# Two cross-attentions in f32 on one core: the second layer's products joint over two pairs of subtiles, and its softmax by head on ScalarE

## The chip, the core and the metric

One core of one Trainium2 chip runs the whole kernel. The metric is the device time of one execution in microseconds (us). The engines are named as in the profile: PE (TensorE, matrix products; PEld is its weight load), DVE (VectorE), ACT (ScalarE), POOL (GpSimd), SP (SyncE, which only issues transfers here). SBUF is the on-chip memory of 128 partitions, PSUM the accumulator memory that PE writes. PSUM holds eight banks of 512 f32 in each partition.

## The reference

x has 4 batches of 1024 tokens, 1024 wide: 4096 rows. ctx has 64 rows a batch, S = 64. All is f32.

```python
# layer 0, 32 query heads on 8 key heads
q, k, v = x @ Wq + bq, ctx @ Wk + bk, ctx @ Wv + bv
attn = softmax(q k^T / sqrt(32) + mask)          # per head
z  = (attn v) @ Wo + bo + x
x1 = layernorm(z, eps=1e-6) * gamma + beta
# layer 1, 16 heads of 64
a = layernorm(ctx, eps=1e-5) * ln_gamma + ln_beta
Q, K, V = x1 @ Wq.T, a @ Wk.T, a @ Wv.T
attn = softmax(where(mask, Q K^T / 8, -inf))     # per head
y = x1 + tanh(gate) * ((attn V) @ Wo.T)
```

## The kernel before

**The folding.** With only 64 context rows, layer 1 needs two square weights per batch: `ad[b]` (1024x1024) is Wq folded with K, so that the scores of all 16 heads are x1 · ad[b], and `bd[b]` is V folded with Wo and the gate, so that y = x1 + p · bd[b], with p the softmax of 16 heads x 64 columns. Both are made during layer 0 and kept in DRAM.

**Winograd's seven products.** Each large product is a one-level Strassen-Winograd product of 2x2 blocks. A subtile is 128 rows; a *pair* is two subtiles (256 rows), whose two subtiles are the two row blocks of the left factor; its 1024 columns, and the weight's rows and columns, are halved. `left_out` makes the left factor's sums S1, S2, S3, S4 on DVE (four instructions of 128x512, lines 429 to 432), `right_sums` those of the weight, T1, T2, T3, N4 (four of 128x2048, lines 183 to 186). `products` then runs seven products, each of four matmuls of 128x512 with f32 (line 446; the trace has two records for one of them), into PSUM banks, and `add` brings each bank to the result in SBUF with a DVE instruction (line 455, or line 459 where the key's mask is added as a bias). `project` runs a list of other work, the `fill`, in seven parts behind the seven steps. In the order of the code the products are:

```python
("X", "A11", "B11", ...), ("X", "S2", "T2", ...), ("V", "S3", "T3", ...), ("X", "S1", "T1", ...),
("X", "S4", "B22", ...), ("V", "A22", "N4", ...), ("W", "A12", "B21", ...)
```

Below they are called P1, P6, P7, P5, P3, P4 and P2 in that order (the same numbers as the changed code has).

**Layer 1.** There are 16 pairs, four a batch. Call S the product that gives a pair's scores, and R the one that gives its y. The order is S0, S1, R0, S2, R1, S3, ..., S15, R14, R15, so that a softmax has an R phase to be made in. For S, the rows x1 come from DRAM by quarters (`load_x1`, SP's queue) in a layout in which DVE's 32x32 stream transpose turns them (`turn_quarters`, line 419), and `left_out` follows. The softmax of a subtile is on DVE: maximum (L493), a clamp (L498), the subtraction of the maximum over 128x1024 (L501), then exp of the whole 128x1024 on ACT (L502), and on DVE the sum (L511), the reciprocal (L512) and the multiplication (L516). p goes to DRAM (`p1`) and comes back by quarters (`turn_p`), both over ACT's queue. For pairs 0 and 15 p is not sent to DRAM: PE turns it by 16 transposes each (`turn_at_once`, line 407) and ACT copies the result (L414). Residual rows x1 are loaded over SP's queue into four buffers `res1`, in which R adds, and y is stored from there.

At each new batch `right_weight` loads a new weight (16 transfers) and DVE makes its four sums: a's in R, b's in S.

**PSUM and order.** `ps_wx` has four single banks, `ps_big` two double ones. Buffers are of pools that rotate: a new tile waits until the last reader of the old one is done. Instructions of each engine run in an order that is fixed when the program is built (a scheduler merges the steps of the code by their dependences); at run time each engine follows its own list and waits on semaphores. DMA issues stand in the lists of the engines that issue them.

**Layer 0 near its end.** `project` of pair 15 is the last product, and then the layer norm of its two subtiles (`close_rows`, `normalize_steps`) and their stores to x1 run as `fill`. `other_work` loads bo for layer 0's GpSimd add of bias and residual rows (L962), and `open_stage` loads gamma and beta. x1[0] and x1[1] are loaded and turned during layer 0's last pairs.

Of the kernel before, what the change touches and what calls it, by code (L numbers as in the profile page):

```python
# [14 lines left out]
P = 128  # L15
# [56 lines left out]
def tile_two_cross_attentions(  # L72
# [27 lines left out]
    def sub_ap(t):  # L100
        return slice(t * P, (t + 1) * P)
# [5 lines left out]
    small = ctx.enter_context(tc.tile_pool(name="small", bufs=4))  # L107
    ps_wx = ctx.enter_context(tc.tile_pool(name="ps_wx", bufs=4, space=bass.MemoryType.PSUM))
    ps_big = ctx.enter_context(tc.tile_pool(name="ps_big", bufs=2, space=bass.MemoryType.PSUM))

# [122 lines left out]
    def constant(ap, shape, name, dt=F32, pool=const):  # L233
        t = pool.tile(shape, dt, tag=name, name=name)
        nc.sync.dma_start(out=t, in_=ap)
        return t
# [5 lines left out]
    beta1_sb = constant(beta1, [P, KC], "beta1")  # L242
    mask1_sb = constant(mask1.partition_broadcast(P), [P, B, S], "mask1", U8)
    gate_sb = constant(gate.partition_broadcast(P), [P, 1], "gate")
# [400 lines left out]
    def load_queries(t):  # L645
        q = qpool.tile([P, KC, P], F32, tag="q", name=f"q0_{t}")
        nc.sync.dma_start(out=q, in_=qTd[t // SUB][:, :, sub_ap(t % SUB)])

        m = small.tile([P, 2, S], F32, tag="m0", name=f"m0_{t}", bufs=2)
        for e in range(2):  # L650
            nc.sync.dma_start(out=m[:, e], in_=mask0[sub_ap(t), :])
        queries[t] = q, m
# [313 lines left out]
    def other_work(rows):  # L966

        nonlocal fold, early, bo_sb, w_o, first, first_rows, second
        for blk in range(1, NBLK):
# [18 lines left out]
        w_o, w_o_loads = right_loads(wo0, "wa", "wo0", "heads")  # L988
        bo_sb = constant(bo0.partition_broadcast(P), [P, H], "bo", F32, fold)
        for k in range(KC):  # L990
# [49 lines left out]
    def open_stage():  # L1040
        nonlocal lpool, o2pool, rpool, gamma0_sb, beta0_sb
        attention.close()
        lpool = open_pool(inner, "left", 1, "right")
        o2pool = open_pool(inner, "o2", 2, "right")
        rpool = open_pool(stage, "res", 6, "right")
        c2 = open_pool(stage, "const2", 1, "right")
        gamma0_sb, beta0_sb = (
            constant(ap.partition_broadcast(P), [P, H], n, F32, c2)
            for ap, n in ((gamma0, "gamma0"), (beta0, "beta0"))
        )  # L1050
# [14 lines left out]

    lefts = {}

    def load_x1(pair):
        xq = xqpool.tile([P, 2 * NQ, QW], F32, tag="xq", name=f"xq1_{pair}")
        load_quarters(xq, x1[pair])  # L1070
        return xq

    def turn_x1(pair, xq, pool=None, tag="xT"):

        xT = (pool or xTpool).tile([P, KC, 2 * P], F32, tag=tag, name=f"xT_{pair}")

        def half(h):
            turn_quarters(xq, xT[:, h * HK : (h + 1) * HK, :], (h * HK, (h + 1) * HK))

        def blocks():  # L1080
            lefts[pair] = left_out(xT, lpool if pool else lxpool, f"x_{pair}")

        return [lambda: half(0), lambda: half(1), blocks]

# [17 lines left out]
    for pair in range(1, NPAIR):  # L1102
# [3 lines left out]
        if pair <= KC:  # L1106
            ahead_w = chunk(wo1, pair, "wo1") if pair < KC else None
            fill += folded_values(vT, wch, pair - 1)
            wch = ahead_w
        if pair == KC + 2:  # L1110
            w_a, w_a_sums = right_weight(ad[0], "wb", "a0", True)
        if pair in (NPAIR - 3, NPAIR - 2):
            fill += w_a_sums[0:2] if pair == NPAIR - 3 else w_a_sums[2:4]
        if pair == 3:
            early_cm.close()
            xTpool = open_pool(last_cm, "x1T", 1)
            lxpool = open_pool(last_cm, "leftx", 1)
            xqpool = open_pool(last_cm, "x1q", 1)
        if pair == NPAIR - 4:
            xq = load_x1(1)  # L1120
        if pair == NPAIR - 3:
            fill += turn_x1(1, xq)

        def tail():
            nonlocal ahead_a
            if pair + 1 < NPAIR:
                ahead_a = left_out(ahead_o, lpool, f"0_{pair + 1}")
            else:
                turned[2]()

        project(a, w_o, r, fill, tail=tail)
        fill = close_rows(pair, r)
        if pair == NPAIR - 2:
            xq = load_x1(0)
            turned = turn_x1(0, xq, o2pool, "o2")
            fill = turned[:2] + fill
    w_b, w_b_sums = right_weight(bd[0], "wa", "b0", True)
    xq = load_x1(2)
    run(fill)
    stage.close()  # L1140


    spool = open_pool(last_cm, "scores1", 4)
    pqpool = open_pool(last_cm, "p1q", 1)
    scores = {}

    def score(pair, fill):
        if pair:
            s = [spool.tile([P, H], F32, tag="s", name=f"s1_{pair}_{u}") for u in range(2)]
        else:  # L1150
            both = o2pool.tile([P, 2, H], F32, tag="o2", name="s1_0")
            s = [both[:, u] for u in range(2)]
        project(lefts.pop(pair), w_a, s, fill, key_bias[:, pair // PPB, :])
        scores[pair] = [su.rearrange("p (h s) -> p h s", s=S) for su in s]

    def softmax1(pair):

        s = scores[pair]
        steps = []
        if pair in (0, NPAIR - 1):  # L1160
            at_once[pair] = pqpool.tile([P, 2, H], F32, tag="pq", name=f"pn_{pair}")
        for u in range(2):
            steps += softmax_front(s[u], True, f"1_{pair}_{u}", pair == 0)
        for u in range(2):
            total, divide = softmax_back(
                s[u], f"1_{pair}_{u}", at_once[pair][:, u] if pair in at_once else None
            )

            def end(u=u, total=total, divide=divide):
                total()  # L1170
                divide()
                if pair not in at_once:
                    nc.scalar.dma_start(
                        out=p1[pair][sub_ap(u), :], in_=s[u].rearrange("p h s -> p (h s)")
                    )

            steps.append(end)
        return steps

    def new_pT(pair):  # L1180
        return ppool.tile([P, KC, 2 * P], F32, tag="pT", name=f"pT1_{pair}")

    def turn_at_once(pair):
        pT = new_pT(pair)
        del scores[pair]
        for u in range(2):
            turn(at_once[pair][:, u], pT[:, :, sub_ap(u)])
        return left_out(pT, lppool, f"p_{pair}")

    probs1 = {}  # L1190
    at_once = {}

    def turn_p(pair):

        scores.pop(pair)
        pq = pqpool.tile([P, 2 * NQ, QW], F32, tag="pq", name=f"pq_{pair}")
        load_quarters(pq, p1[pair], nc.scalar)
        pT = new_pT(pair)

        def half(h):  # L1200
            turn_quarters(pq, pT[:, h * HK : (h + 1) * HK, :], (h * HK, (h + 1) * HK))

        def blocks():
            probs1[pair] = left_out(pT, lppool, f"p_{pair}")

        return [lambda: half(0), lambda: half(1), blocks]

    score(0, w_b_sums)
    score(1, softmax1(0))
    inner.close()  # L1210
    ppool = open_pool(last_cm, "probsT1", 1, "right")
    lppool = open_pool(last_cm, "leftp", 1, "right")
    rpool = open_pool(last_cm, "res1", 4, "right")
    probs1[0] = turn_at_once(0)
    for pair in range(NPAIR):
        r = []
        for u in range(2):
            ru = rpool.tile([P, H], F32, tag="r", name=f"r1_{pair}_{u}")
            nc.sync.dma_start(out=ru, in_=x1[pair][sub_ap(u), :])
            r.append(ru)  # L1220
        fill = []
        if pair + 2 < NPAIR:
            fill += turn_x1(pair + 2, xq)
        if pair + 1 < NPAIR:
            fill += softmax1(pair + 1)
        if (pair + 2) % PPB == 0 and pair + 2 < NPAIR:
            b = (pair + 2) // PPB
            w_a, w_a_sums = right_weight(ad[b], "wb", f"a{b}", True)
            fill += w_a_sums
        project(probs1.pop(pair), w_b, r, fill)  # L1230
        if (pair + 1) % PPB == 0 and pair + 1 < NPAIR:
            b = (pair + 1) // PPB
            w_b, w_b_sums = right_weight(bd[b], "wa", f"b{b}", True)
        else:
            w_b_sums = []
        for u in range(2):
            nc.sync.dma_start(out=y[(pair * 2 + u) * P : (pair * 2 + u + 1) * P, :], in_=r[u])
        if pair + 3 < NPAIR:
            xq = load_x1(pair + 3)
        if pair + 2 < NPAIR:  # L1240
            score(pair + 2, w_b_sums[:3] + turn_p(pair + 1) + w_b_sums[3:])
        elif pair + 1 < NPAIR:
            probs1[pair + 1] = turn_at_once(pair + 1)
    last_cm.close()
    fold_cm.close()

# [54 lines left out]
```

## Time and profile before

| | |
|---|---|
| runs of the kernel | 1909.1, 1907.62, 1908.9 us; median 1908.9 |
| profiled execution, first to last instruction (span) | 1909.7 us; the profile has no other time of it, so that this is taken as its own time, 0.8 us above the median |
| busy in the span: PE / DVE / ACT / POOL | 98% / 68% / 22% / 9% |
| granted clock of TensorE, mean | 0.994 |
| layer 1, from its first product | 1126.3 us to the end, 783 us |
| busy of DVE in layer 1 | 509 of 783 us |
| busy of ACT and POOL in layer 1 | 39 and 0 of 783 us |

How to read it: a line of the groups is "line engine operation out<-in shapes xcount | busy us, mean ns of one | idle time of the engine just before, and what ended it". Names have their buffer numbers left out, so that `a_B` stands for the blocks of all ad weights. A line of waits is "engine tile line <- engine tile line that released it: us in total, times, longest". A line of the timeline is "start us, us, what, [idle before <- releaser]". DVE's mean duration of an instruction is some 80 ns more than its pitch in a row of them.

### The profile page before, as it was taken

To read this page: it belongs to the slowest core of one execution; us is meant where nothing else is said; L and a number is where in the kernel's file an instruction comes from. 1 tells how busy PE (TensorE), PEld (TensorE's weight loads), DVE (VectorE), ACT (ScalarE), POOL (GpSimd) and SP (SyncE) were. 2 spreads that over 40 slices of the span, in tenths; PEclk is the share of its full clock that TensorE was granted. 3 is DMA by queue.
4 is the path that set the end of the run, shared out by engine and by line. 5 is a ranking of instruction groups with operands and counts; after the bars stand their busy time and mean duration, and the time that the engine had idled before them with its cause. 6 is when DMAs were issued, how large, how long until landed. Compare 5 with 4: busy or idle time off the path is not lost.

```text
span 1909.7 us, 17518 instructions
## 1 busy us (share of the span) xinstructions
PE 1865.5 (98%) x6096; PEld 879.6 (46%) x6096; DVE 1290.2 (68%) x1582; ACT 427.4 (22%) x1396; POOL 178.5 (9%) x212
## 2 busy tenths in 40 slices
PE   8999999999998899999999999999999999999999
PEld 7744444444445653343344444444444444444444
DVE  3425589789888985575568668557665766576653
ACT  1101575766546741212200001000000000000000
POOL 0016011111101003121113100000000000000000
PEclk9999999999999899999999999999999999999999
DMA  8996599998868965667473362466656565656421
GB/s 278 184 222 192 159 266 241 272 248 272 250 178 290 305 234 173 196 201 242 167 215 136 121 149 82 110 165 162 146 143 165 154 155 143 165 145 164 121 88 44
DMA packets 220745, 350.54 MB, mean 184 GB/s; under 512 B 26992, under 2 KB 146160, under 8 KB 215664
## 3 DMA queue, kind: packets, MB, share of 16 engines
q1 hardware_dynamic: 152896, 242.44, 45.8%
q0 software_dynamic: 15216, 60.83, 10.4%
q10 hardware_dynamic: 52544, 46.14, 8.7%
q8 instruction: 48, 0.79, 0.2%
q14 instruction: 41, 0.34, 0.1%
HBM read 207.53 MB, written 141.82 MB: 183 GB/s over the span
## 4 chain that ended last, share of the span: by engine, by line
PE 80%; DVE 9%; DMA 5%; ACT 3%; issue 2%; POOL 0%; SPq 0%; DVEq 0%; ACTq 0%; POOLq 0%
PE wx L446 59%; PE wx L576 12%; ACT s L698 2%; PE big L680 2%; DVE s L684 2%; PE wx L379 1%; PE big L379 1%; PE big L928 1%; DVE mx L691 1%; DVE s L715 1%; DMA q<-qTd 1%; DMA pq<-p 1%; DMA p<-s 1%; PE big L759 1%; DVE sm L711 1%
## 5 line engine op out<-in xcount | busy, mean ns | idle before, releaser
L455 DVE TENSOR_TENSOR r<-wx,r 128x512 f32<-128x512 f32 x224 | 153.3, 685 | 234.1 <-PE wx L446 218.1
L698 ACT ACTIVATE s<-s,mx 128x64 f32<-128x64 f32 x488 | 162.7, 336 | 80.4 <-DVE mx L691 77.3
L502 ACT ACTIVATE s<-s 128x1024 f32<-128x1024 f32 x32 | 33.7, 1057 | 651.7 <-DVE s L501 651.6
L459 DVE TENSOR_TENSOR s<-wx,key_bias 128x512 f32<-128x512 f32 x64 | 44.1, 689 | 136.8 <-PE wx L446 136.8
L446 PE MATMUL wx<-wo_B,S 128*128 128x512 f32 x256 | 116.8, 599 | 1.5 <-DVE r L455 1.5
L576 PE MATMUL wx<-xT,wq_S 128*128 128x512 f32 x256 | 116.6, 598 | 0.8 <-ACT z L587 0.8
L446 PE MATMUL wx<-b_B,pT 128*128 128x512 f32 x256 | 115.8, 593 | 0.6 <-ACT pT L414 0.6
L446 PE MATMUL wx<-b_B,S_p 128*128 128x512 f32 x256 | 116.0, 596 | 0.0
L446 PE MATMUL wx<-a_B,xT 128*128 128x512 f32 x256 | 115.4, 592 | 0.0
L446 PE MATMUL wx<-a_B,S_x 128*128 128x512 f32 x256 | 115.3, 593 | 0.1
L446 PE MATMUL wx<-wo_B,o 128*128 128x512 f32 x256 | 114.8, 596 | 0.0
L576 PE MATMUL wx<-xB,wq_A 128*128 128x512 f32 x256 | 113.7, 594 | 0.0
L962 POOL TENSOR_TENSOR r<-r,bo 128x1024 f32<-128x1024 f32 x30 | 77.7, 2597 | 317.7 <-DMA r<-in_x_dram 240.5
L680 PEld LDWEIGHTS big<-kv,q 64*128 64x128 f32 x1024 | 69.6, 194 | 49.2 <-issue 41.3
L684 DVE TENSOR_TENSOR s<-big,m 128x1024 f32<-128x1024 f32 x64 | 77.5, 1215 | 21.6 <-PE big L680 21.2
L698 ACT ACTIVATION_READ_ACCUMULATOR s<-s,mx 128x1 f32 x488 | 91.8, 188 | 0.0
L680 PE MATMUL big<-kv,q 64*128 64x128 f32 x1024 | 81.7, 291 | 1.9 <-DMA q<-qTd 1.8
L419 DVE STREAM_TRANSPOSE pT<-pq 128x1024 f32<-128x1024 f32 x66 | 78.0, 1219 | 5.0 <-DMA pq<-p 4.9
L446 PEld LDWEIGHTS wx<-wo_B,S 128*128 128x128 f32 x256 | 47.2, 190 | 67.7 <-issue 52.1
L715 DVE TENSOR_TENSOR s<-s,sm 128x1024 f32<-128x1024 f32 x64 | 77.0, 1216 | 0.9
L299 ACT ACTIVATE rstd<-rstd 128x1 f32<-128x1 f32 x32 | 6.5, 203 | 316.1 <-DVE rstd L298 316.1
L446 PEld LDWEIGHTS wx<-wo_B,o 128*128 128x128 f32 x256 | 47.8, 190 | 63.5 <-issue 62.4
(162 smaller groups left out, 2936.3 us busy)
## 6 DMA issues: line engine op xcount, KB each, us to landing
p<-s POOLq DMA_DIRECT2D x19, 1024.0 KB, 8.1
pq<-p POOLq DMA_DIRECT2D x76, 256.0 KB, 6.1
xq<-in_x_dram SPq DMA_DIRECT2D x64, 256.0 KB, 9.9
q<-qTd SPq DMA_DIRECT2D x32, 512.0 KB, 7.3
oTd<-oT ACTq DMA_DIRECT2D x32, 512.0 KB, 7.6
ad<-a POOLq DMA_DIRECT2D x16, 1024.0 KB, 8.6
o<-oTd SPq DMA_DIRECT2D x16, 1024.0 KB, 5.3
r<-in_x_dram SPq DMA_DIRECT2D x32, 512.0 KB, 5.3
```

The source lines that it names most:

```text
L379: nc.tensor.matmul(ps[:, 0:256], w[k // HK, c // HK][:, k % HK, sub_ap(c % HK)], ct[:, k, :], start=(k == 0), stop=(k == KC - 1),)
L419: return nc.vector.transpose(dst.rearrange("p k (u i) -> p k u i", i=Q), t[:, :, k0 * Q : k1 * Q].rearrange("p u (k j) -> p k u j", j=Q),)
L446: nc.tensor.matmul(banks[name], a[s][:, k, :], w[m][:, k, :], start=first and k == 0, stop=last and k == HK - 1, skip_group_check=True,)
L455: nc.vector.tensor_tensor(at, bank, at, ALU.add)
L459: nc.vector.tensor_tensor(at, bank.rearrange("p (h s) -> p h s", s=S), bias.unsqueeze(1).to_broadcast([P, 512 // S, S]), ALU.add,)
L502: nc.scalar.activation(s, s, AF.Exp)
L576: nc.tensor.matmul(bank, w_q[a][:, k, sub_ap(i)], rows[b][:, k, :], start=first and k == 0, stop=last and k == HK - 1, skip_group_check=True,)
L680: nc.tensor.matmul(ps[:, at : at + P], q[on, c * 4 + g, :], k0bd[on, b, c, :], start=True, stop=True,)
L684: nc.vector.tensor_tensor(quarters[:, :, c * 8 : (c + 1) * 8], ps.rearrange("p (k a l) -> p a k l", a=NQ, l=Q), mask.rearrange("p e (h l) ...
L698: nc.scalar.activation(heads[:, e, k], heads[:, e, k], AF.Exp, bias=mx[:, e, k : k + 1], accum_out=sm[:, e, k : k + 1],)
L715: nc.vector.tensor_tensor(heads[:, e], heads[:, e], wide(sm[:, e]), ALU.mult)
L962: nc.gpsimd.tensor_tensor(ru, ru, bo_sb, ALU.add)
```

## The change

Layer 1 is done by *quads* of two pairs, called P and Q: eight quads, phases S0, S1, R0, S2, R1, ..., S7, R6, R7. In all but R7 (which is two `project` as before), a phase is `phase` and `go`:

- Four of the seven products stay as they are for each pair: P1, P7, P6, P5 and Q1, Q7, Q6, Q5.
- The other three, A12·B21 ("a"), S4·B22 ("b") and A22·N4 ("c"), are made for both pairs jointly: the left factors of P and Q, one under the other, and the weight block form 2x2 blocks again (left blocks of two 128x128, right ones of 128 x 2 x 256), which get seven products of their own. One such *joint step* (c1, c6, c7, c5, c3, c2, c4, and the same for a and b) is two matmuls of 128x256. A phase has 8 large products and 21 joint steps where before two pairs had 14 large products.
- Their half sums, four T of 128x512 and four S of 128x256 for each of a, b and c, are made by GpSimd in every phase (L1257, L1261), from pools `sumsR` and `sumsL` of six buffers.
- Each joint product is brought to the rows by DVE: three takes of 128x256 (L1279) and two of 128x512 (L1285). P7 and P5 are added in R by one instruction of 1024 (L1208), in S by two (L1202 with the mask's bias, L1200 without).
- The order in a phase is written out in `ORDER`; the last four steps (`REST`) of a phase come in the next one, and its y rows are stored after b3.
- Softmax: DVE keeps the negated maximum and a clamp, ACT makes 16 exps of 128x64 with that bias and the sum by accumulation (L1374); the reciprocal and the multiplication stay on DVE. p is stored over ACT's queue, and reloaded over SP's. No p is turned on PE.
- Rows are loaded and turned by subtile (`turned_rows`), their sums made per pair. Scores and residual rows share four buffers `rows` of two subtiles.
- PSUM in layer 1: two single banks and three double ones.
- In layer 0, bo is loaded in `open_stage` with gamma and beta; x1[0] is loaded and turned at pairs 12 and 13, x1[1] in S0; the pools for the mask and for m0 are other ones.

The core of the diff (the fills of each phase, the pools and the details of banks are cut):

```diff
-    ps_wx = ctx.enter_context(tc.tile_pool(name="ps_wx", bufs=4, space=bass.MemoryType.PSUM))
-    ps_big = ctx.enter_context(tc.tile_pool(name="ps_big", bufs=2, space=bass.MemoryType.PSUM))
...
+    ps_wx = open_banks("ps_wx1", 2)
+    ps_big = open_banks("ps_big1", 3)
+    lb2 = open_pool(last_cm, "leftB2", 2, "right")
+    rpool = open_pool(last_cm, "rows", 4, "right")
+    jrpool = open_pool(last_cm, "sumsR", 6, "right")
+    jlpool = open_pool(last_cm, "sumsL", 6)
+
+    BIG, INNER = 3.43, 0.86
+    JOINT = {"a": ("A12", "B21", 0, 0), "b": ("S4", "B22", 0, 1), "c": ("A22", "N4", 1, 0)}
...
+            def rsum(o, x, y, rb=rb, j=j):
+                rb[o] = jrpool.tile([P, 2, 256], F32, tag="jr", name=f"{o}_{j}")
+                nc.gpsimd.tensor_tensor(rb[o], rb[x], rb[y], sub)
+
+            def lsum(o, x, y, op, lb=lb, j=j):
+                lb[o] = jlpool.tile([P, 2, P], F32, tag="jl", name=f"l{o}_{j}")
+                nc.gpsimd.tensor_tensor(lb[o], lb[x], lb[y], op)
+
+            def mm(key, a, b, first, last, lb=lb, rb=rb, ps=ps):
...
+                for k in range(2):
+                    nc.tensor.matmul(
+                        ps[key], lb[a][:, k, :], rb[b][:, k, :],
+                        start=first and k == 0, stop=last and k == 1, skip_group_check=True,
+                    )
...
+            def take(key, i, c, ps=ps, out=out):
+                at = out(i, c, c + 1)
+                nc.vector.tensor_tensor(at, ps[key], at, add_)
...
+    ORDER = (
+        "cT1 cT2 cT3 cN4 aT1 aT2 P1 | - | P7 | - | P6 Q1 P5 "
+        "cb ab bb cS1 cS2 cS3 cS4 aS1 aS2 c1 c2 Q7 c6 aT3 aS3 c7 aN4 aS4 Q6 c4 bT1 Q5 c5 bS1 bT2 "
+        "a1 a2 c3 bS2 a6 bT3 bS3 b1 a7 bN4 bS4 b2 b6 a4 a5 b7"
+    ).split()
+    REST = "a3 b4 b5", "b3"
...
+        def front():
+            nc.vector.tensor_reduce(mx, v, AX.X, ALU.max, negate=True)
+            nc.vector.tensor_scalar(mx, mx, -LEAST_MAX, None, ALU.min)
+            for h in range(16):
+                nc.scalar.activation(
+                    v[:, h], v[:, h], AF.Exp, bias=mx[:, h : h + 1], accum_out=sm[:, h : h + 1]
+                )
+
+        def back(to):
+            nc.vector.reciprocal(sm, sm)
+            nc.vector.tensor_tensor(v, v, sm.unsqueeze(2).to_broadcast([P, 16, S]), ALU.mult)
+            nc.scalar.dma_start(out=to, in_=s[:, u])
...
+                if n % QPB == 0:
+                    w_b, loads = right_loads(bd[n // QPB], "wa", f"b{n // QPB}", True)
+                    fill += [(8.0, f) for f in loads]
+                    fill += [(24.0 + 5.0 * k, f) for k, f in enumerate(right_sums(w_b))]
```

The numbers that stand with the fills (8.0, 24.0 + 5k) are places in the phase's code, in PE's time as the code counts it (`BIG`, `INNER`); where an instruction stands in its engine's list is settled by the scheduler.

## The prediction

> **What bounds the kernel now.** First the busy shares, then layer 1 in stretches of 100 us, then what TensorE (PE) waits for there. From the page, parts 1 and 4:
>
> ```profile
> span 1909.7 us, 17518 instructions
> PE 1865.5 (98%) x6096; PEld 879.6 (46%) x6096; DVE 1290.2 (68%) x1582; ACT 427.4 (22%) x1396; POOL 178.5 (9%) x212
> PE 80%; DVE 9%; DMA 5%; ACT 3%; issue 2%; POOL 0%; SPq 0%; DVEq 0%; ACTq 0%; POOLq 0%
> ```
>
> PE is busy nearly all the time and carries the chain. Layer 1 begins at 1126.3 us, with the first product on a_B. The table of stretches (busy us of PE, weight load, DVE, ACT, POOL, then the granted clock) and PE's waits from 1125 us on:
>
> ```profile
> 1326.00:1426.00 100.00, 100.00 (x233) 43.92 (x233) 68.94 (x86) 4.23 (x4) 0.00 (x0) 1.00 0.61 152
> 1626.00:1726.00 100.00, 100.00 (x233) 43.74 (x232) 68.30 (x86) 4.23 (x4) 0.00 (x0) 1.00 0.63 158
> PE wx L446 <- DVE pT L431: 0.7, 1, 0.7
> PE wx L446 <- ACT pT L414: 0.6, 2, 0.4
> ```
>
> For 783 us PE waits 1.3 us in all. So two things only matter here: how much PE work goes, and whether PE still never waits. VectorE (DVE) has 31 us of slack in 100; GpSimd (POOL) is unused.
>
> **PE work removed.** The timeline has one product of four 128x512 matmuls (8 records), and in layer 0 one of eight 128x256 (16 records), each with the next row's start behind it:
>
> ```profile
> 1126.33 3.60 PE L446 MATMUL wx<-a_B,xT 128*128 128x512 f32 x8
> 1129.76 1.88 PE L446 MATMUL wx<-a_T,xT 128*128 128x512 f32 x4
> 31.34 3.62 PE L379 MATMUL big<-ctxT,wk 128*128 128x256 f32 x16
> 34.80 1.46 PE L379 MATMUL wx<-ctxT,wk 128*128 128x256 f32 x6
> ```
>
> A product takes 1129.76 - 1126.33 = 3.43 us. Half as wide a matmul takes (34.80 - 31.34)/8 = 0.432 us, half of 3.43/4 = 0.857, so small tiles cost PE nothing extra; a joint step of two is 0.863 us. A quad's phase is 14 products now, 48.0 us. After: 8 products (27.4) and 3 x 7 joint steps (18.1) = 45.6. The 15 phases on the new path (S0 to S7, R0 to R6) save 2.45 x 15 = 36.7 us; the last R phase is as before. The PE transposes of pairs 0 and 15 go too: 32 of them, 3.8 us busy, and the 1.3 us of waits. Together **-41.8 us**, fairly sure.
>
> **What DVE gets.** Durations (and pitches back to back) from the groups: 128x512 685 ns (0.60 us), 128x1024 1218 (1.135), reduction 1201 (1.126), transpose 1218 (1.158; a half 0.59), 128x256 416 (0.335), 128x2048 2280 (2.20).
>
> ```profile
> L455 DVE TENSOR_TENSOR r<-wx,r 128x512 f32<-128x512 f32 x113 | 77.3, 684 | 82.6 <-PE wx L446 82.3
> L501 DVE TENSOR_TENSOR s<-s,mx 128x1024 f32<-128x1024 f32 x32 | 39.0, 1218 | 0.3
> L511 DVE TENSOR_REDUCE sm<-s 128x16 f32<-128x1024 f32 x32 | 37.6, 1204 | 0.0
> L520 DVE TENSOR_TENSOR pn<-s,sm 128x256 f32<-128x256 f32 x16 | 5.7, 416 | 0.0
> L183 DVE TENSOR_TENSOR b_B<-b_B,b_B 128x2048 f32<-128x2048 f32 x4 | 9.1, 2280 | 0.0
> ```
>
> Per subtile it loses the subtraction and the sum (2.26 us; 9.0 a quad), and gains the joint adds: each of the three products, in each phase, takes 3 x 0.335 + 2 x 0.60 = 2.2 us where two adds took 1.2. All operations counted, a quad is some 61 us before and 64 after, of 91.2 us of PE. In the mean DVE keeps its slack. But its order is fixed when the program is built, and PE now has only 2 single banks and 3 double ones, with short steps of 0.86 us; what counts is what stands on DVE ahead of an add that PE waits for. I added the pitches along DVE's built order, from the last PE product that holds it to the add that frees a bank, plus 0.35 us for the way there and back, and took off the PE work that is queued meanwhile.
>
> **Waits added.** (1) *S0.* Behind the last add of layer 0, DVE's order has pair 1's turn and four left sums (3.6 us), the layer norm of two subtiles (four statistics 2.4, four passes 4.6, small ones 0.7) and all four sums of b's weight (8.8; wanted only from R0 on), 20.1 us; then S0's first add, which PE needs before P6. With the last add of layer 0, that add and the way there and back 20.1 + 0.6 + 0.6 + 0.35 = 21.6; PE has P1, P7 and three joint steps, 9.4. **12.2 us.** (2) *S2, S4, S6.* Before the adds of Q1 and Q7 come two transposes and four left sums of p (3.6 us). From b1: 0.34 + 3.6 + 3 x 0.60 + 0.34 + 0.35 = 6.4, less 1.4 of PE: **5.0 each.** (3) *S3, S5, S7.* In that place stand the next b weight's sums T2, T3, N4, 6.6 us: 9.4 - 1.4 = **8.0 each.** (4) *R2, R4.* With the next a weight's sums between the joint adds: 7.4 us (a sum of 2.2, a wide add 1.14, others 4.1) less 3.9 before a7 = 3.5; N4 before b4 1.8; next phase's c1 behind the turn of its x, 2.1: **7.4 each.** (5) *R0 and start of S2.* 1.6 + 0.95 + 3.7, where S2's P1 waits for its own turn: **6.3.** Sum: 12.2 + 15.0 + 24.0 + 14.9 + 6.3 = **+72.4 us.** The same addition on before's order finds nothing over 0.1 us, as PE's 1.3 us of waits say.
>
> None of it is paid back: after a wait PE is again the slower one, but its time is gone. Bounds: the order can't change, so the waits shrink only if neighbours overlap more than the rows' pitches show, to half (36 us) at the least; above, late data adds what stands under the next heads.
>
> **The clock.** PE gaps cost more than themselves, in layer 0:
>
> ```profile
> 720.14 5.40 PE L446 MATMUL wx<-wo_T,S 128*128 128x512 f32 x8 [2.24 <-DVE r L455]
> 718.00:722.00 4.00, 1.86 (x3) 0.83 (x4) 0.69 (x1) 0.00 (x0) 4.00 (x3) 0.88 0.50 167
> 722.00:726.00 4.00, 4.00 (x8) 1.77 (x7) 0.36 (x1) 0.00 (x0) 1.97 (x1) 0.70 0.59 196
> ```
>
> After a gap of 2.24 us the clock fell and the product took 5.40 in place of 3.60: 1.8 us. I charge this to the seven waits of 5 us and more: **+12.6 us**. Ends: 0 (slowed PE work lets DVE catch up before the next shortage) and 13 gaps at twice 1.8, 47. The Trainium skill ("TensorE: Matmul & The Clock Gate", Part 1) has half rate after an idle window of about 3.4 us, in windows that do not start with the work; by that a 2.24 us gap would be safe, which the row contradicts, and only the seven long waits would pay, some 3.4 us at half clock, 1.7 each.
>
> **GpSimd.** 12 sums of 128x512 and 12 of 128x256 a phase. The 128x1024 add L962 takes 2.35 us undisturbed, so about 1.2 and 0.65: 22 us of 45.6, and its order has a shortage of 0.2 us at b6 only. Speaking against the change: such adds slow DVE instructions that read two SBUF tiles, and are slowed.
>
> ```profile
> 727.28 1.27 DVE L306 SCALAR_TENSOR_TENSOR r<-r,mv,gamma 128x1024 f32<-128x1024 f32 x1
> 727.76 6.31 POOL L962 TENSOR_TENSOR r<-r,bo 128x1024 f32<-128x1024 f32 x2 [3.80 <-DMA r<-in_x_dram]
> 729.26 2.60 DVE L309 SCALAR_TENSOR_TENSOR r<-r,rstd,beta 128x1024 f32<-128x1024 f32 x1
> ```
>
> L309 takes 1.28 us alone, 2.60 beside it. The skill ("SBUF — State Buffer", Who interferes with whom) says one of the two blocks fully for the other's whole instruction; PSUM adds have one SBUF input and are spared. In layer 1 left sums, right sums and the softmax product read SBUF alone: in an S and R pair about 30 us of DVE at most meet GpSimd at work half the time. Cover: DVE's 30% slack, and half sums made before their step. I take +2 us; ends 0 and +20 (each of eight pairs delays one step by a 2.2 us sum).
>
> **The rest, with one answer: nothing.** Exp by head on ScalarE: 336 ns, some 5.3 us a subtile, 21 of 91 us, from the row L698 of layer 0. p is now reloaded over SP's queue, behind x1 rows, weights and y stores; p<-s took 2.7 and pq<-p 5.2 us to land, and the turn comes over 10 us later; if a load comes late, DVE stands, and PE after it: up to 10 us, in the range. The y stores issue after b3; the buffers are wanted 15 us later, landing takes 5.5. Loading bo with gamma and beta in layer 0 (6 and 9.5 us) lies where GpSimd waits for rows: 0, ends -2 and +3.
>
> **Sum.** 1909.7 - 41.8 + 72.4 + 12.6 + 2 = 1954.9, in the profiled execution's span, which is 0.8 above the median of 1908.9: **1954**. I take 1950, as waits close together can share a price.
>
> **Rivals.** *Faster.* DVE's waits are mostly absent, because its adds overlap more and sums arrive in gaps my addition does not see: PE's 2.45 us a phase stays. With S0's 12 us and a third of the other 60 (20), and no clock loss, 1908.9 - 41.8 + 32 = 1899; with a sixth, 1889. For it: DVE has 30% of slack, and before shows that a full PE is possible. Against: the order of each engine is fixed and the weight sums of 2.2 us stand ahead of adds wherever they do. It decides when the sum of waits is under 42 us. *Slower still.* The shared port and late p loads come on top, the clock falls at every gap: 1954 + 20 + 15 = 1989. For it: L309's row; against: layer 1's adds from PSUM are free of it. *No gain from halves* (the change doesn't save PE time): if joint steps cost 1.0 rather than 0.863, 21 x 15 x 0.14 = +43; the row L379 speaks against, since its weight load (190 ns) fits in its pitch of two records (432).
>
> **Chances.** Forecast's case (1925 to 1970) 0.50; faster 0.25; slower still or halves dear 0.20; near the old time 0.05. The range cuts the last tenth on each side: 1885 to 1990. 0.2% (4 us) is what a measurement can tell from no change: faster 0.26, same 0.04, slower 0.70.
>
> **What would show it.** PE's waits in layer 1 should be named "<- DVE" at the bias adds (L1202) and takes (L1279), with one of about 12 us at S0 and three near 8; a phase without waits should have a PE busy time of 45.6 us; granted clock under 1 behind long gaps. Wrong if PE's waits there stay under 42 us in all, if joint steps have a pitch well over 0.86, or if POOL and DMA are the names behind the waits.

## The result, and the profile after

The changed kernel takes 2019.7 us (median of four runs, 2016.4 to 2024.8) against 1909.0: ratio 1.058, interval 1.056 to 1.060. The forecast had the sign and the places of the waits, but 1950 and at most 1990 for the size. Its profiled execution has a span of 2023.0 us.

From the page of the changed kernel, parts 1 and 2:

```profile
span 2023.0 us, 20595 instructions
PE 1874.4 (93%) x6604; PEld 987.3 (49%) x6604; DVE 1380.1 (68%) x1741; ACT 561.5 (28%) x2384; POOL 595.1 (29%) x572
...
PEclk9999999999999989999999899999899998999899
```

PE's busy time is 9 us more than before although 42 us of its work are gone: part of its work now runs at half the clock (a row below has 0.50). DVE's share is the same 68%. The view of PE's waits from 1125 us on, the seven largest of eleven lines:

```profile
PE wx L1189 <- DVE s L1202: 46.5, 7, 17.9
PE joint L1269 <- DVE r L1279: 17.6, 10, 4.4
PE wx L1189 <- DVE r L1208: 8.7, 6, 1.9
PE joint L1269 <- DVE s L1279: 5.7, 10, 1.1
PE joint L1269 <- POOL T_a L1257: 4.8, 6, 0.8
PE joint L1269 <- DVE tb L426: 4.2, 2, 2.1
PE wx L1189 <- issue: 3.6, 1, 3.6
...
```

All eleven come to 99 us, where before had 1.3. The names are those that were forecast: bias adds (L1202) and takes (L1279) on DVE. Two stretches of the after-trace, S0's start and R2's end, show both costs (same columns as in the table of before):

```profile
1150.00:1200.00 50.00, 34.52 (x94) 18.53 (x94) 37.25 (x43) 1.28 (x1) 24.90 (x17) 0.80 0.20 53
1500.00:1550.00 50.00, 41.12 (x132) 25.77 (x131) 31.68 (x40) 6.36 (x39) 24.69 (x18) 0.93 0.34 100
```

PE is busy 35 and 41 us of 50, at a granted clock of 0.80 and 0.93 where before had 100 of 100 at 1.00.

For each run below three numbers are worked out from the trace: where layer 1 starts (its first product); the idle time of PE in layer 1 (all gaps between its records, up to 1 us more than the view of waits has); and the *slow excess* there, the time between PE's record starts beyond the undisturbed 0.429 us (128x512) or 0.22 us (128x256), gaps left out. The kernels narrow_sums and reorder_narrow compute joint products of half sums that are mostly zeros, so that they are bounds and no versions.

| kernel | median us | ratio to before, interval | layer 1 starts | layer 1 lasts | PE idle | slow excess |
|---|---|---|---|---|---|---|
| before | 1909 | | 1126 | 783 | 1.3 | 4 |
| changed | 2019.7 | 1.058 (1.056-1.060) | 1138 | 885 | 99 | 39 |
| narrow_sums | 1968.7 | 1.031 (1.028-1.033) | 1135 | 837 | 66 | 29 |
| pin_sums | 1985.1 | 1.039 (1.037-1.041) | 1133 | 850 | 74 | 30 |
| dve_half | 1990.5 | 1.043 (1.041-1.044) | 1132 | 858 | 78 | 37 |
| left4 | 1990.0 | 1.042 (1.040-1.043) | 1134 | 854 | 79 | 32 |
| reorder | 1938.7 | 1.015 (1.014-1.017) | 1126 | 812 | 47 | 23 |
| reorder_narrow | 1888.3 | 0.989 (0.988-0.991) | 1129 | 762 | 13 | 11 |
| reorder_left4 | 1907.2 | 0.999 (0.998-1.000) | 1125 | 781 | 26 | 15 |
| tuned | 1912.0 | 1.001 (1.000-1.002) | 1126 | 783 | 25 | 16 |

The bill of the changed kernel, in its profiled execution: 11 us late at layer 1 (1137.7 for 1126.3); then 783 - 42 = 741 of work, 99 idle, 39 slow, 6 unaccounted (probably bits of pitch at the gaps' ends), 885.

### The profile page after: what moved, and what is told of

Read it like the earlier page. It is cut to its first block, busy times and chain, and to the rows that moved or that the text cites. A ratio compares the mean times of both kernels' runs of the same rounds, so it can differ in the third digit from the quotient of the medians.

```text
span 2023.0 us, 20595 instructions
## 1 busy us (share of the span) xinstructions
PE 1874.4 (93%) x6604; PEld 987.3 (49%) x6604; DVE 1380.1 (68%) x1741; ACT 561.5 (28%) x2384; POOL 595.1 (29%) x572
## 5 line engine op out<-in xcount | busy, mean ns | idle before, releaser
L1374 ACT ACTIVATE s<-s,mx 128x64 f32<-128x64 f32 x512 | 170.0, 334 | 618.2 <-DVE mx L1372 618.1
L462 DVE TENSOR_TENSOR r<-wx,r 128x512 f32<-128x512 f32 x126 | 86.1, 686 | 173.5 <-PE wx L453 170.8
L705 ACT ACTIVATE s<-s,mx 128x64 f32<-128x64 f32 x488 | 162.6, 335 | 80.8 <-DVE mx L698 77.8
L1374 ACT ACTIVATION_READ_ACCUMULATOR s<-s,mx 128x1 f32 x512 | 96.0, 187 | 0.0
L705 ACT ACTIVATION_READ_ACCUMULATOR s<-s,mx 128x1 f32 x488 | 91.6, 188 | 0.0
L1189 PE MATMUL wx<-a_T,S 128*128 128x512 f32 x112 | 63.8, 703 | 29.2 <-DVE s L1202 28.6
L746 POOL DMA_DIRECT2D pq<-p x76 | 41.6, 554 | 162.7 <-DVE pT L426 66.3
L865 POOL DMA_DIRECT2D wq1T<-wq1c x64 | 35.0, 554 | 149.2 <-DVE wq1c L426 148.0
L583 PEld LDWEIGHTS wx<-xB,wq_A 128*128 128x128 f32 x256 | 48.1, 190 | 58.7 <-issue 56.9
L583 PEld LDWEIGHTS wx<-xT,wq_S 128*128 128x128 f32 x256 | 47.4, 190 | 59.0 <-issue 55.2
```

The costliest lines, as they stand in the source:

```text
L462: nc.vector.tensor_tensor(at, bank, at, ALU.add)
L583: nc.tensor.matmul(bank, w_q[a][:, k, sub_ap(i)], rows[b][:, k, :], start=first and k == 0, stop=last and k == HK - 1, skip_group_check=True,)
L705: nc.scalar.activation(heads[:, e, k], heads[:, e, k], AF.Exp, bias=mx[:, e, k : k + 1], accum_out=sm[:, e, k : k + 1],)
L746: nc.gpsimd.dma_start(out=pq[a * Q : (a + 1) * Q], in_=v[a])
L1189: nc.tensor.matmul(banks[key, i], left[i][s][:, k, :], w[m][:, k, :], start=first and k == 0, stop=last and k == HK - 1, skip_group_check= ...
L1374: nc.scalar.activation(v[:, h], v[:, h], AF.Exp, bias=mx[:, h : h + 1], accum_out=sm[:, h : h + 1])
```

## Experiments

Theory A: the order of VectorE's list makes the waits, shared reads of SBUF by GpSimd and VectorE lengthen them, and half clock behind the gaps adds to each. Rivals: shared reads alone (B); shared reads matter nothing to PE (C); VectorE has too much to do (D).

**GpSimd's reads taken away.** In the changed kernel:

```diff
-                nc.gpsimd.tensor_tensor(rb[o], rb[x], rb[y], sub)
+                nc.gpsimd.memset(rb[o][:, :, 8:], 0.0)
+                nc.gpsimd.tensor_tensor(rb[o][:, :, 0:8], rb[x][:, :, 0:8], rb[y][:, :, 0:8], sub)
```

and the same for the left half sums.

> The changed kernel with GpSimd's half sums made only 8 columns wide and the rest filled with zeros, which reads no SBUF (the joint products are computed of wrong halves). VectorE's and TensorE's orders are in effect unchanged. Theory A (the order of VectorE's list gives the waits, the shared reads of SBUF a part, the clock another): DVE's left sums go back from 0.92-0.99 us to 0.69, S0's wait from 17.9 to about 12.5 us, the unforeseen gaps of R0 (3.5 and 1.2) and R2, R4 (2.5 more than summed) vanish; idle of PE in layer 1 from 97 to about 75 us; time 2020 -> 1990 to 2000. Theory B (the shared reads are the main cost): idle falls below 40, time below 1950. Theory C (the shared reads matter nothing to PE): within 5 us of 2020.

Measured: 1968.7, 51 us less: idle 33 us less, slow excess 10 less, layer 1 begins 3 earlier, and some 5 unaccounted. Left sums and the softmax product, groups of layer 1 (changed kernel, then this one):

```profile
L1380 DVE TENSOR_TENSOR s<-s,sm 128x1024 f32<-128x1024 f32 x32 | 48.8, 1526 | 1.0
L1107 DVE TENSOR_TENSOR S<-S,ta 128x512 f32<-128x512 f32 x30 | 29.7, 989 | 0.7
```

```profile
L1382 DVE TENSOR_TENSOR s<-s,sm 128x1024 f32<-128x1024 f32 x32 | 39.2, 1224 | 1.0
L1107 DVE TENSOR_TENSOR S<-S,ta 128x512 f32<-128x512 f32 x30 | 20.6, 688 | 0.7
```

0.99 us back to 0.69, and 1.53 to 1.22. One of the weight sums ahead of S0's first add, likewise:

```profile
1158.02 3.23 DVE L192 TENSOR_TENSOR b_T<-b_T,b_B 128x2048 f32<-128x2048 f32 x1
```

```profile
1151.38 2.29 DVE L192 TENSOR_TENSOR b_T<-b_T,b_B 128x2048 f32<-128x2048 f32 x1
```

S0's wait, on the timeline of PE, first in the changed kernel and then without the reads:

```profile
1165.18 6.53 PE L1189 MATMUL wx<-a_T,S_x 128*128 128x512 f32 x8 [17.87 <-DVE s L1202]
```

```profile
1156.56 5.59 PE L1189 MATMUL wx<-a_T,S_x 128*128 128x512 f32 x8 [12.09 <-DVE s L1202]
```

12.09 us, where the addition of pitches in the prediction had 12.2. The waits that the addition did not have went (3.5 and 1.2 in R0, 1.9 each in R1, R3, R5), and R2's and R4's first fell from 4.4 to 3.4, summed 3.5. The waits of 6.2 us in S3, S5 and S7 are the same in both. All of layer 1 has 66 us of idle, against 72 summed. So the addition was nearly right for a VectorE that is left alone, and GpSimd's reads make the other third; 4.8 us of it are waits for GpSimd's own sums (T_a above), which the edit also makes shorter. Of the theories A stands, but its price for shared reads, 20 to 30 us, was too small. B's and C's numbers both fail.

**Weight sums held at their place.** DVE's three sums of b stand together in the changed kernel; its timeline in S3:

```profile
1447.67 2.28 DVE L191 TENSOR_TENSOR b_T<-b_B,b_B 128x2048 f32<-128x2048 f32 x1
...
1449.98 2.29 DVE L192 TENSOR_TENSOR b_T<-b_T,b_B 128x2048 f32<-128x2048 f32 x1
1452.19 2.29 DVE L193 TENSOR_TENSOR b_N<-b_B,b_T 128x2048 f32<-128x2048 f32 x1
1455.13 2.08 PE L1189 MATMUL wx<-a_T,S 128*128 128x512 f32 x2 [6.20 <-DVE s L1202]
1457.00 2.07 PE L1269 MATMUL joint<-T_c,lS_c 128*128 128x256 f32 x4
```

Six us of DVE, six of PE's wait, and then joint steps of 2.07 us that take 1.03 elsewhere: the half clock, which the view of that stretch has as 0.50 (same columns as above):

```profile
1455.10:1458.50 3.40, 3.37 (x6) 1.75 (x7) 1.84 (x4) 0.00 (x0) 0.00 (x0) 0.50 0.21 40
```

The edit:

```diff
-            lambda: tt(r["T1"], r["T1"], r["B11"], ALU.subtract),
+            lambda: behind(tt(r["T1"], r["T1"], r["B11"], ALU.subtract)),
```

and so for all four, where `behind` adds the scheduler's edge to the instruction traced before on the engine.

> The changed kernel with each weight sum (T1, T2, T3, N4) held behind the DVE instructions that stand before it in the code, so that no three of them stand together ahead of an add. Theory A (order): the waits of 6.2 us in S3, S5, S7 fall to about 2, S0's by 2 to 3, and three clock drops with them: 15 us of idle and 5 to 10 of clock less, 2020 -> 1993 to 2003. Theory B (shared reads of SBUF) and D (DVE simply has too much to do): the sums take as long wherever they stand, the waits come elsewhere; within 6 us of 2020.

Measured: 1985.1, 35 us less; in the profiled executions 41 (2023.0 and 1982.3), of which idle 26, slow excess 9, and layer 1 begins 5 earlier. The waits of 6.2 are 1.5 now, S0's 17.9 is 10.2:

```profile
1152.29 5.17 PE L1195 MATMUL wx<-a_T,S_x 128*128 128x512 f32 x8 [10.15 <-DVE s L1208]
...
1439.66 1.13 PE L1275 MATMUL joint<-T_c,lS_c 128*128 128x256 f32 x4 [1.48 <-DVE s L1285]
```

The same sums, the same VectorE load, other places: D falls, A holds, with a gain above its 17 to 27.

**Half sums on VectorE.** `nc.gpsimd` became `nc.vector` in the two lines.

> The changed kernel with all half sums on VectorE instead of GpSimd (result unchanged): no shared reads at all, but 11 us more of VectorE a phase, 86 of 91 us a quad. By the pitches waits of 93 us, 14 more than with GpSimd undisturbed. Theory A: shared reads cost 33 us of idle in the changed kernel, so idle 97 -> 90 to 95 and the time 2010 to 2025. Rival (VectorE's load is the bound): 2050 or more.

Measured: 1990.5, 29 us less than the changed kernel, though VectorE has 22 us more of work a quad. S0 waits 14.9 us. The same two groups as above, now with GpSimd idle in layer 1 and whole half sums:

```profile
L1380 DVE TENSOR_TENSOR s<-s,sm 128x1024 f32<-128x1024 f32 x32 | 38.8, 1212 | 0.2
L1107 DVE TENSOR_TENSOR S<-S,ta 128x512 f32<-128x512 f32 x30 | 20.4, 679 | 0.2
```

Both expectations were missed: idle is 78 us and not A's 90 to 95, the time is 20 us under A's 2010, and the rival's 2050 is far off. The addition of pitches, 93 us here, was 15 too long. So on this order GpSimd's help costs more than it brings.

**Left sums on GpSimd too**, in the changed kernel's order:

```diff
-            tt(left["S1"], left["S3"], left["A22"], ALU.add)
...
+            g[0](left["S1"], left["S3"], left["A22"], ALU.add)
...
```

Here `g[0]` is GpSimd's instruction in layer 1; S2, S3 and S4 are changed in the same way.

> The changed kernel, in its own order of phases, with the four left sums of each pair on GpSimd too. By the pitches 86 us of waits where the changed kernel has 79, since GpSimd takes 1.27 us a sum and PE waits for S2 and c6; shared reads are left only for the softmax product and the weight sums. Theory A (order first; shared reads 33 us of idle and 10 of clock): idle 97 -> 85 to 95, time 2000 to 2015. Rival (taking the left sums off VectorE is what made the reordered kernel as fast as before, whatever the order): 1985 or less.

Measured: 1990.0, 30 us less; just short of the rival's 1985, and under A's range. Taking the left sums off VectorE is worth as much as putting the half sums there, even with GpSimd's slower sums. By the pitches alone the waits should have grown (86 us for 79), so that the lighter VectorE does not explain the gain; that it comes from fewer collisions is argued, as the softmax product and the weight sums still collide. But without the order it does not reach before.

**The order changed.** `behind` for the weight sums; y rows of pair Q stored after b5 rather than b3; other places of loads and turns; `sumsR` opened ahead of the other pools, so that S0's rows lie off the rows that x1's last stores read; bo loaded twice, once early:

```diff
+                if rest[1]:
+                    rest[1](1 - part)
...
-                fill += turn_fill(p1[2 * n], p_lefts, n, 0, 3.0, 17.5, 0)
...
+                fill += turn_fill(p1[2 * n], p_lefts, n, 0, 1.0, 20.0, 0)
...
-                    fill += [(24.0 + 5.0 * k, f) for k, f in enumerate(right_sums(w_b))]
...
+                    fill += [(20.0 + 5.0 * k, f) for k, f in enumerate(right_sums(w_b))]
```

> The changed kernel with the same instructions in another order: weight sums held behind their place in the code, y rows of pair Q stored a phase part earlier, other places of loads, turns and sums in the phases, the pools of layer 1 laid so that S0's rows do not wait for x1's last stores, and bo loaded early as before for the first pairs of layer 0. By the pitches along VectorE's list, without shared reads, some 22 us of waits are left of the 72 to 79. Theory A (order, then shared reads, then clock): idle of PE 97 -> 35 to 50, slow-clock excess 39 -> 15 to 20, layer 0 some 7 us earlier; 2020 -> 1920 to 1940. Theory B (shared reads alone matter): 1990 or more. It is also the candidate for a kernel faster than before: that needs under 1908.

Measured: 1938.7, idle 47, slow excess 23 (15 to 20 expected), layer 1 at 1126: A's time, and still 1.5% slower than before. What each of these edits is worth by itself was not tried, but for the weight sums (above) and bo (below).

**Both causes taken away.**

> The kernel 'reorder' with GpSimd's half sums 8 columns wide and zeros for the rest (joint products of wrong halves), so that both causes are taken away at once. If order and shared reads are the whole of the idle time, PE waits some 20 us in layer 1, the clock loses under 10, and the time is 1126 + 741 + 30 = 1890 to 1905, faster than before; if a third cause is there (DMA, ScalarE, small matmuls), over 1915.

Measured: 1888.3, idle 13, slow 11. Both causes together leave no room for a third one of size: the time is 1.1% under before, and layer 1 lasts 762 us against 783.

**Order, and left sums on GpSimd.**

> The kernel 'reorder' with the four left sums of each pair on GpSimd too (32 us of GpSimd in 45.6 a phase, VectorE 10 us a quad less), so that of the instructions that meet on SBUF's shared reads mainly the softmax product and the weight sums are left on VectorE. Pitches give 34 us of waits, now for GpSimd (c6 of S2, S4, S6 4.7 us each). If shared reads cost more than that, as theory A says (33 us in the changed kernel), it is 5 to 15 us faster than 'reorder'; if GpSimd's chain is the new bound, slower by 10 or more.

Measured: 1907.2, ratio 0.9988 (0.9978 to 0.9997), some 31 us less than 'reorder' where 5 to 15 were expected. Its waits in layer 1:

```profile
PE wx L1199 <- DVE a_T L196: 8.9, 3, 3.0
PE joint L1279 <- POOL lS_c L1271: 4.8, 3, 1.8
PE joint L1279 <- POOL lS_b L1271: 3.4, 4, 1.1
...
```

What is left is one weight sum (T2 of a) that lies behind S2's, S4's and S6's first add, and GpSimd's length. This is the best full version: as fast as before, or 2 us faster, at the edge of what can be told apart.

**Its places shifted again.** The numbers of the fills only.

> The kernel 'reorder_left4' with other places of x's and p's loads and turns in the phases; by the pitches 28.5 us of waits instead of 34. If the pitches tell what is left there, idle 26 -> 20 us and the clock some 3 us less: 1898 to 1903, faster than before by 0.3 to 0.6%. Rival (what is left are shared reads of the softmax product and GpSimd's length): 1905 to 1910, the same.

Measured: 1912.0 (1.0008, interval 0.9999 to 1.0017), nearest the rival's case. Five us fewer of waits by the pitches were no gain in the run (idle 25 for 26): with these few waits the pitches no longer rank two orders.

**Two parts of the change alone, in the kernel before.** First the softmax by head (16 exps with bias and accumulated sum on ACT, no subtraction and no sum on DVE):

> The kernel before with only the softmax changed: 16 exps by head on ACT with accumulated sums, DVE without the subtraction and the sum. All theories: DVE loses some 72 us of layer 1, PE is 100% busy there before and after, so 1909 within 3 us. Rival: DVE standing for ACT's 5.3 us a subtile delays adds, as in R1, R3, R5 of the changed kernel: 8 waits of 2 us or more, 1920 to 1940.

Measured: 1911.3, 1.0007 (0.9996 to 1.0019). 72 us less of DVE work are worth nothing where DVE was not late, and ACT does no harm. Then bo's load alone, moved into `open_stage`:

> The kernel before with only bo's load moved to where gamma and beta are loaded. Theory: GpSimd's and DVE's first adds of bo wait for it (it landed 8.4 us after its issue in the changed kernel), and PE waits twice for 2 to 3 us and runs at half clock behind: 1909 -> 1915 to 1920. Rival: the 11 us that the changed kernel is late at layer 1's start come from its other edits of layer 0 (x1's turn at pairs 12 and 13, the pools): within 3 us of 1909.

Measured: 1917.1, 1.0036 (1.0025 to 1.0048): 6.6 us. Its timeline:

```profile
713.52 0.42 SPq L235 DMA_DIRECT2D bo<-in_bo_dram  x1
722.58 1.23 DVE L1098 TENSOR_TENSOR r<-r,bo 128x1024 f32<-128x1024 f32 x1 [6.10 <-DMA bo<-in_bo_dram]
726.78 3.70 PE L446 MATMUL wx<-wo_T,S 128*128 128x512 f32 x8 [3.11 <-DVE r L455]
```

DVE stands 6.1 us for the transfer, and PE 3.1 (and 2.3 once more). Of the 11 us that the changed kernel loses before layer 1, bo explains 4 to 7 (layer 1 begins 4 us later in this run). The rest was not tried by itself; 'reorder', which has bo early and another order in layer 1, has none of it.

## Why the prediction was wrong in size

- **PE work, -41.8 us: right.** A joint step takes what was summed; from the timeline of the changed kernel in R0, four steps in a row begin 0.86 us apart:

```profile
1285.58 1.03 PE L1269 MATMUL joint<-T_c,lS_c 128*128 128x256 f32 x4
1286.44 1.03 PE L1269 MATMUL joint<-b_B,tb 128*128 128x256 f32 x4
1287.30 1.03 PE L1269 MATMUL joint<-b_B,S 128*128 128x256 f32 x4
1288.17 1.03 PE L1269 MATMUL joint<-N_c,tb 128*128 128x256 f32 x4
```

- **Waits by the order of VectorE, +72.4: nearly right, when nothing else slows VectorE** (66 in narrow_sums). By place, summed and in the changed kernel: S0 12.2 and 17.9; S2, S4, S6 5.0 and 4 to 5; S3, S5, S7 8.0 and 7.5; R2, R4 7.4 and 9.9; R0's end 6.3 and 6.8. Not foreseen: 4.7 at R0's start and 2.7 in each of R1, R3, R5.
- **Shared reads of SBUF, +2 with an end of +20: the step that failed most.** The term was priced at +2; without GpSimd's reads the kernel has 33 us less of idle and 10 less of slow clock, with 3 us before layer 1 and 5 unaccounted 51 in all. The mechanism was seen (L309's row), and the Trainium skill ("SBUF — State Buffer", Who interferes with whom) was borne out: the instructions of two SBUF inputs are longer, L1279's adds from PSUM stayed at 415 ns, where a 128x256 sum of before had 416. What was wrong was the cover. "DVE's 30% slack" is a mean over a phase; the prediction had itself found that in front of certain adds there is none, and there each longer instruction goes into PE's wait one for one. S0's pile is mostly such instructions (left sums, passes of the layer norm, weight sums: 15.8 of the 20.1 us), and GpSimd begins its sums just there: 5.8 us on that one wait.
- **The clock, +12.6 with an end of 47: too small.** The slow excess rose by 35 us (39 against 4). It was charged to the seven longest waits at 1.8 us. Over eight of the traces (those of the table but left4 and tuned), a gap of 4 us or more was followed by slow time each time (16 of 16, 2.8 us in the mean), one of 2 to 4 us in 33 of 47 (mean 1.6), one of 0.5 to 2 us in 10 of 133. The changed kernel has eleven gaps over 3 us and two of 2.1. The skill's rule of an idle window of about 3.4 us ("TensorE: Matmul & The Clock Gate", Part 1) is a fair guide to the size; as a threshold it is too high here, since 26 of those 33 gaps were shorter than that.
- **bo, 0 with ends -2 and +3: wrong.** GpSimd and DVE waited for the transfer; 6.6 us in the kernel before.
- **ScalarE, nothing: nearly right.** In the changed kernel DVE stands 27.6 us for exps, and in R1, R3, R5 it lies ahead of a wait of PE of 1.9 us. Without GpSimd's reads PE has no such wait.
- **The range.** The upper ends of the terms, 72 + 20 + 47 + 3 on 1909.7 - 41.8, give 2010; with the late loads' 10, 2020. That this is the time measured is chance: shared reads went past their end, the clock stayed under its own, and no transfer is among the names that DVE or PE waits for in layer 1. But the range was cut as if the ends were independent, and they are not: a longer VectorE instruction makes a longer gap, and that a slower clock (10 us less of it in narrow_sums).
- **The rivals.** The faster one failed where it said it would: its waits had to stay under 42 us. The slower one, 1989, had the right names, shared reads and the clock, but 35 us for them and late loads on top. Dear halves are out: a joint step's pitch is 0.86 us.

## What to carry to other kernels

Before work is given to an idle engine, ask which instructions of the busy one become longer beside it (here those of two SBUF inputs), and look for the places where the busy one has no slack: the price is paid there, not out of the mean. In the changed kernel's order, putting left sums and half sums on one engine (the left sums to GpSimd, or the half sums to VectorE) was worth 30 us in either direction, more than sharing them out. Where an engine has one fixed list, add up what stands ahead of each result that the bound engine needs; that sum found the places, and where nothing collided it was too long each time (72 us in the prediction and 79 in a later count for 66 measured, 93 for 78 in dve_half, 22 for 13 in reorder_narrow). A gap on TensorE has also to be charged with the slow time behind it.

## What the runs showed of the hardware

- GpSimd is slowed too: its 128x512 sum takes 1.27 us in the changed kernel where no instruction of DVE overlaps it, and 2.25 in the mean in this group, beside which the softmax product L1380 runs each time:

```profile
L1257 POOL TENSOR_TENSOR T_b<-b_B 128x512 f32<-128x512 f32 x7 | 15.8, 2251 | 0.0
```

- A small one-input instruction is touched as well: the clamp L1372 (128x16, one SBUF input) takes 350 ns in the mean in the changed kernel, 263 in narrow_sums and 156 in dve_half, where GpSimd is idle. The mean hides two kinds: in the changed kernel eight of the 32 take 0.43 to 1.05 us, each with a GpSimd instruction beside it, and the others 0.13 to 0.18, none with one.
- In reorder_left4, with 36 us of GpSimd in the stretch from 1150 to 1200 us, PE is busy 49.8 of the 50 at a clock of 1.00: there, GpSimd at work does not harm PE by itself.
